# Context attention with heads in row groups, and projections and norms moved in among the steps of self-attention

## The chip, the cores and the metric

The kernel runs on one core of one Trainium2 chip. The metric is the device time of a whole execution in microseconds (us), as the median of several runs: 6629.17 us for the kernel before (3 runs, 6628.52 to 6630.94).

## The reference

A decoder of four layers, pre-norm, in float32. The state x has 2 batches of 1024 tokens of 256 features; a context has 2 batches of 154 tokens. Each layer has three stages, each added onto x: a token mixer, a stage that reads the context, and a feed-forward stage. Four stages are touched by the change. Three hold a self-attention of 16 heads of 16 features:

```python
# L0_attn (causal; keys and values through a latent of 64)
c_kv = x @ W_DKV
k = (c_kv @ W_UK).reshape(b, t, h, hd); v = (c_kv @ W_UV).reshape(b, t, h, hd)
q = (x @ W_UQ).reshape(b, t, h, hd)
probs = softmax(where(causal, einsum('bqhd,bkhd->bhqk', q, k) / sqrt(hd), -inf))
return einsum('bhqk,bkhd->bqhd', probs, v).reshape(b, t, d) @ W_O

# L2_ffn: h = x + attention(rmsnorm(x, ln1_w)); then a mixture of experts on h
# L3_ffn: attention on a layer norm with gain and bias, biases on q, k, v and output;
#         then a mixture of experts
```

The fourth is the context attention of layer 1, 16 heads of 16 features, queries from x, keys and values from the context's 154 tokens:

```python
# L1_xattn: Q = layernorm(x), K = V = ctx
q, k, v = split_heads(Q, Wq, bq), split_heads(K, Wk, bk), split_heads(V, Wv, bv)
attn = softmax(einsum('bhqd,bhkd->bhqk', q, k) / sqrt(d_k), axis=-1)
out = einsum('bhqk,bhkd->bqhd', attn, v).transpose(0, 2, 1, 3).reshape(B, Sq, d_model)
return out @ Wo.T + bo
```

## The kernel before, in words

x stays in SBUF as 16 tiles of 128 tokens (NT = 16; BT = 8 tiles a batch). The program is one list of stages, and each stage takes its tile pools, works and releases them. Inside `attention` a manual schedule holds: each engine's instructions run in the order in which the code issues them.

**Self-attention, `attend` (line 564).** A loop over two batches. For each batch, one after the other: `normed` computes the norm of the batch's eight tiles on VectorE (statistics L250, L251; square root on ScalarE L258; reciprocal; scaling L262 or L264) and turns them with 16 transposes on TensorE (L276), evacuated at L280, L282 or by `evac` (L229 on ScalarE and L233 on VectorE in turn). `heads_T` (line 550) then projects queries and keys, transposed: 8 + 8 groups `hT` of 512 tokens, one for each block `ch` of 128 rows, in which each of four heads has 32 rows (16 features, a row for the maximum, and zeros). L0_attn projects its latent `c` before. Eight value tiles `pv` follow. All of them are matmuls recorded under `mm`, L239.

Then comes `attention` (line 357), with the softmax in two passes. It works in eight steps: two blocks of 512 queries times four groups `ch` of four heads. For each step, the A pass computes scores `sa` with queries on the partitions (L387; one head uses 32 of TensorE's 128 rows) and takes their maxima on VectorE (L416). `m_columns` (L424, L426) puts the negated maxima into a tile M, and `m_rows` (four transposes L432, an add L434) puts them as an extra row beside the queries, so that the B pass's scores `sb` (keys on the partitions, L387) already have the maximum subtracted. ScalarE takes the exponential into `pT` (L447), in the causal stage GpSimd clears the upper triangle (L450), and the value matmuls (L461) accumulate `o`, copied to `oT` (L466). After the last group of a query block, four `finish` calls transpose, divide by the sums and project the output (L340, L342, L344, L318, then `po` L239, and the add to x L326).

The order is written by hand. All of step 0's maxima and four more pairs go ahead of the first B score; this stretch is called the lead below. Then the A pairs of step i + 1 are spread between the B pairs of step i. A tick follows each pair, and a list `due` counts ticks down for what comes later:

```python
LEAD, LAG, KB, FIN, STEP, GAP = 4, 3, 2, 3, 1, 2
...
first = len(a_items(0)) + LEAD
while na < first:
    it = a_next()
    a_matmul(it, 0)
    a_matmul(it, 1)
    tick()
```

Scores of both passes share a pool of seven PSUM banks; `o` has one bank. `pT` has six buffers.

**Context attention, `context_attention` (line 1088).** It serves L1_xattn and L3_xattn. It norms all 16 tiles, projects queries into two blocks of 128 rows (eight heads of 16 features each), and writes keys block-diagonally into `kbd` (L1116, L1118): a key block holds one head's 16 rows and zeros elsewhere. Then it runs over 64 units, a token tile times a group of four heads, in a software pipeline: `front` computes scores `s` (L1148, two matmuls of 128x308, two heads each, over all 128 rows), the maximum (L1160), the subtraction (L1161) and the exponential (L1162); `middle`, two units later, transposes the weights `p` (L1171, eight transposes in two tiles `pt`) and copies them to `pT`; `back` multiplies by the values (L1181, eight matmuls into 32 rows each). `finish` is the same as above. GpSimd adds the output bias to x in `add_row` (L299).

Of the kernel before, what the change touches and what calls it, by code (L numbers as in the profile page):

```python
# [8 lines left out]
F32 = mybir.dt.float32  # L9
# [62 lines left out]
def _blocks(f):  # L72
# [15 lines left out]
    for i in range(2):  # L88
# [8 lines left out]
    g = "L1_xattn_"  # L97
    put("b4", q=_kp(f[g + "Wq"].T), k=_kp(f[g + "Wk"].T), v=_kp(f[g + "Wv"].T), o=_kp(f[g + "Wo"].T),
        bq=_col(f[g + "bq"]), bk=_col(f[g + "bk"]), bv=_row(f[g + "bv"]), bo=_row(f[g + "bo"]))
    g = "L1_ffn_"  # L100
# [73 lines left out]
class Model:  # L174
# [110 lines left out]

    def normed(self, pool, psum, eps=1e-5, g=None, b=None, rms=False, src=None, twice=False, t0=0, n=NT):

        xT = pool.tile([P, 2, n * P], F32, name="xT")
        with self.tc.tile_pool(name="xn", bufs=1) as xp:
            xn = xp.tile([P, n, D], F32, name="xn")  # L290
            self.norm(xp, (self.x if src is None else src)[:, t0 : t0 + n, :], xn, n, eps, rms)
            if twice:
                self.norm(xp, xn, xn, n, eps, rms)
            self.transposed(psum, xn, xT, n, g=g, b=b)
        return xT
# [60 lines left out]

    def attention(self, b, qT, kT, v, causal, wo, x):

# [12 lines left out]
        with ExitStack() as c:  # L371
            pool = lambda name, bufs, **kw: c.enter_context(tc.tile_pool(name=name, bufs=bufs, **kw))
            sb = pool("att", 2)
            pa = pb = pool("att_a", 7, space=PSUM)
            po_pool = pool("att_o", 1, space=PSUM)
            steps = [(qb, ch) for qb in range(S // QB) for ch in range(4)]
            M = []
            for i in range(2):
                m = sb.tile([P, QT, P], F32, name=f"M{i}", bufs=1)
                nc.gpsimd.memset(m, 0.0)  # L380
                M.append(m)
            nk = lambda qb: (qb + 1) * QT if causal else BT
            mms, pTs, os, oTs = {}, {}, {}, {}
# [5 lines left out]
            def a_items(i):  # L389
                qb, ch = steps[i]  # L390
                out = []
                for t in range(QT):
                    qt = qb * QT + t
                    n = (qt + 1) * P if causal else S
                    for half, k0 in enumerate(range(0, n, 512)):
                        for hp in range(2):
                            out.append((i, t, half, k0, min(n, k0 + 512), hp, (n + 511) // 512))
                return out
# [5 lines left out]
            def a_matmul(item, j):  # L404
                i, t, half, k0, k1, hp, halves = item
                qb, ch = steps[i]
                if i not in mms:
                    mms[i] = self.small.tile([P, QT, 2, 4], F32, name="mm", bufs=3)
                n, h = k1 - k0, 2 * hp + j
                s = pa.tile([P, 512], F32, name="sa", tag="sb")[:, :n]  # L410
                q0 = (qb * QT + t) * P
                score(s, qT, kT, h, ch, q0, q0 + P, k0, k1)
                if causal and half == halves - 1:
                    d = s[:, n - P :]
                    nc.vector.tensor_tensor(d, d, self.c["tri"], ALU.add)
                nc.vector.tensor_reduce(mms[i][:, t, half, h : h + 1], s, AX.X, ALU.max, negate=True)  # L416

            def m_columns(i):
# [3 lines left out]
                cols = m.rearrange("p t (j r) -> p t j r", j=4)[:, :, :, DH]  # L422
                if causal and qb == 0:
                    nc.vector.tensor_copy(cols, mm[:, :, 0, :])  # L424
# [11 lines left out]
            def b_matmul(item, j):  # L436
# [4 lines left out]
                if j == 0 and hp == 1:  # L441
                    pTs[i, kc] = sb.tile([P, 4, QB], F32, name="pT", bufs=6)
                h = 2 * hp + j
                s = pb.tile([P, QB], F32, name="sb", tag="sb")
                score(s[:, :n], kT, qT, h, ch, kc * P, kc * P + P, q0, q0 + n)
                p = pTs[i, kc]
                nc.scalar.activation(p[:, h, :n], s[:, :n], AF.Exp)  # L447
                if causal and kc * P >= qb * QB and j == 1:
# [3 lines left out]
            def values(i, kcs):  # L452
# [4 lines left out]
                for kc in kcs:  # L457
                    p = pTs.pop((i, kc))
                    n = (qb + 1) * QB - max(qb * QB, kc * P) if causal else QB
                    for j in range(4):  # L460
                        nc.tensor.matmul(os[i][32 * j : 32 * j + 32, QB - n :], v[:, kc, 4 * ch + j, :], p[:, j, :n],  # L461
                                         start=kc == 0, stop=kc == last)
# [21 lines left out]

            LEAD, LAG, KB, FIN, STEP, GAP = 4, 3, 2, 3, 1, 2
            A = [it for i in range(len(steps)) for it in a_items(i)]
# [24 lines left out]

            with tc.manual_schedule():
                first = len(a_items(0)) + LEAD
                while na < first:
                    it = a_next()
                    a_matmul(it, 0)
                    a_matmul(it, 1)
                    tick()
                goal = first
                for i, (qb, ch) in enumerate(steps):  # L520
# [3 lines left out]
                    for g, bi in enumerate(B):  # L524
                        goal = base + share * (g + 1) // len(B)
                        its = []
                        while na < min(goal, len(A)):
                            its.append(a_next())
                        it = its[0] if its else None
                        for j in range(2):  # L530
                            if it:
                                a_matmul(it, j)
                            b_matmul(bi, j)
                        for it in its[1:]:
                            a_matmul(it, 0)
                            a_matmul(it, 1)
                        if g % 2:
# [25 lines left out]

    def attend(self, name, make, wq, wk, wv, wo, x, causal=False, bq=None, bk=None, bv=None):

        nc, tc = self.nc, self.tc
        for b in range(B):
            with ExitStack() as c:  # L570
                sb = c.enter_context(tc.tile_pool(name=f"{name}{b}", bufs=1))
                qT = sb.tile([P, 4, S], F32, name="qT")
                kT = sb.tile([P, 4, S], F32, name="kT")
                v = sb.tile([P, BT, H, 32], F32, name="v")
                nc.gpsimd.memset(v, 0.0)
                nc.gpsimd.memset(v[:, :, :, DH], 1.0)
                with tc.tile_pool(name=f"{name}{b}p", bufs=3, space=PSUM) as psum, tc.tile_pool(name=f"{name}{b}x", bufs=1) as xp:
                    qs, kv = make(b, xp, psum)
                    kparts = kv[0].shape[0]
                    self.heads_T(psum, qT, wq, qs, 0, S, 0.25, bq)  # L580
                    self.heads_T(psum, kT, wk, kv, 0, S, None, self.c["one16"] if bk is None else bk, kparts)
                    for t in range(BT):
                        pv = psum.tile([P, D], F32, name="pv", tag="tp")
                        self.mm(pv, [(xk[:, t * P : t * P + P], w[:kparts]) for xk, w in zip(kv, wv)])
                        pvh = pv.rearrange("p (h d) -> p h d", h=H)
                        if bv is None:
                            self.evac(v[:, t, :, :DH], pvh)
                        else:
                            nc.vector.tensor_tensor(v[:, t, :, :DH], pvh, bv.rearrange("p (h d) -> p h d", h=H), ALU.add)
                self.attention(b, qT, kT, v, causal, wo, x)  # L590

    def of_normed(self, **kw):


        def make(b, pool, psum):
            xT = self.normed(pool, psum, t0=b * BT, n=BT, **kw)
            chunks = [xT[:, k, :] for k in range(2)]
            return chunks, chunks

        return make  # L600

    def L0_attn(self):
        w = self.weights("b0")

        def make(b, pool, psum):
            xT = self.normed(pool, psum, t0=b * BT, n=BT)
            ckv = pool.tile([64, S], F32, name="ckv")
            for t0 in range(0, S, 512):  # L610
                ps = psum.tile([64, 512], F32, name="c", tag="tp")
                self.mm(ps, [(w["dkv"][:, k * 64 : k * 64 + 64], xT[:, k, t0 : t0 + 512]) for k in range(2)])
                self.evac(ckv[:, t0 : t0 + 512], ps)
            return [xT[:, k, :] for k in range(2)], [ckv]

        self.attend("l0a", make, [w["uq"][:, :512], w["uq"][:, 512:]], [w["uk"]], [w["uv"]], w["o"], self.x, causal=True)

# [585 lines left out]
    def L1_xattn(self):  # L1203
        self.context_attention(self.weights("b4"))

# [56 lines left out]
    def L2_ffn(self):  # L1262
# [3 lines left out]
        with tc.tile_pool(name="l2f", bufs=1) as sb:  # L1266
            h = sb.tile([P, NT, D], F32, name="h0")
            with tc.tile_pool(name="l2f_n", bufs=1) as np_:
                self.norm(np_, self.x, h, NT, 1e-5)
            self.attend("l2f", self.of_normed(src=h, rms=True, g=w["g1"]), cut(w["q"]), cut(w["k"]), cut(w["v"]), w["o"], h)  # L1270
            self.L2_experts(w, h)
# [313 lines left out]
    def L3_ffn(self):  # L1585
# [3 lines left out]
        with ExitStack() as top_stack:  # L1589
# [6 lines left out]
            with tc.tile_pool(name="l3f_n", bufs=1) as np_:  # L1596
                self.norm(np_, self.x, x1, NT, 1e-5)
            self.attend("l3f", self.of_normed(src=x1, g=w["g1"], b=w["b1"]), cut(w["q"]), cut(w["k"]), cut(w["v"]), w["o"], x1,
                        bq=w["bq"], bk=w["bk"], bv=w["bv"])
# [470 lines left out]
```

## Time and profile before

| what | value |
|---|---|
| median of 3 runs | 6629.17 us |
| profiled execution: its own time | 6639.63 us |
| profiled execution: span in the trace | 6637.7 us |
| TensorE (PE) busy | 5827.5 us, 88% of the span |
| VectorE (DVE) busy | 3994.5 us, 60% |
| ScalarE (ACT) busy | 2786.3 us, 42% |
| GpSimd (POOL) busy | 1462.3 us, 22% |
| L0_attn, latent of batch 0 to its first B score | 16.04 to 60.33 us |
| L1_xattn, first transpose to last output projection | 2103.47 to 2354.71 us |
| L2_ffn batch 0, first transpose to last output projection | 3828.63 to 4131.46 us |
| L2_ffn, first projection of batch 1 | 4142.77 us |
| L3_ffn, last output projection of batch 0, first projection of batch 1 | 5945.45, 5955.44 us |

The profile is one execution. Its span is the time from the first to the last instruction in the trace, and 1.9 us of the execution lie around it. A line "L387" is line 387 of the kernel before; a helper's line collects all stages that call it, so a stage is picked out by a window of time or by the names of the tiles. "out<-in" names the tiles of an instruction, "128*128 128x512" the weights and the moving operand of a matmul. A float32 matmul leaves two records. "[0.61 <-DVE v L233]" behind a group is the idle time before it and the instruction that ended that time. PEclk is the TensorE clock that was granted, as a share of full speed.

### The profile page before, as it was taken

The numbers are of one execution on the slowest core, as the hardware profiler recorded it, in microseconds if no ns is written. First come the engines' busy times: TensorE is split into PE (matmuls) and PEld (weight loads), VectorE is DVE, ScalarE is ACT, GpSimd is POOL, SyncE is SP. The second block draws the span as 40 slices with busy tenths as digits, with TensorE's granted clock in tenths as the row PEclk, the third lists the DMA queues.
The fourth block names the chain that finished last, engine by engine and source line by source line (L and its number), as shares of the span: only waits on it lengthen the run. The fifth ranks groups of instructions, "written<-read, shape, count | busy, mean of one in ns | idle before, by whom it ended". The sixth has DMA issues, their size and how long they took to land.

```text
span 6637.7 us, 79839 instructions
## 1 busy us (share of the span) xinstructions
PE 5827.5 (88%) x30196; PEld 3190.3 (48%) x30196; DVE 3994.5 (60%) x7906; ACT 2786.3 (42%) x5377; POOL 1462.3 (22%) x1095
## 2 busy tenths in 40 slices
PE   8898999999998987787878799988687987999896
PEld 4445656565644653333324544445444445444464
DVE  7665545454556735998983365652376778657521
ACT  3344545454501416787762035441133433354411
POOL 1110000000002005998992100001323133000012
PEclk8899999999988998998989789988878898999888
DMA  1000000000000003554551000011100000000022
GB/s 38 1 1 15 1 1 1 14 1 1 1 10 23 1 14 98 143 146 130 151 150 44 13 1 1 1 64 67 53 1 13 1 6 16 1 1 1 13 84 94
DMA packets 112621, 234.88 MB, mean 35 GB/s; under 512 B 12965, under 2 KB 37133, under 8 KB 108525
## 3 DMA queue, kind: packets, MB, share of 16 engines
q1 hardware_dynamic: 97872, 194.73, 10.0%
q0 software_dynamic: 6480, 17.70, 0.9%
q10 hardware_dynamic: 7884, 17.34, 0.7%
q8 instruction: 239, 3.92, 0.2%
q14 instruction: 146, 1.19, 0.1%
HBM read 211.51 MB, written 18.22 MB: 35 GB/s over the span
## 4 chain that ended last, share of the span: by engine, by line
PE 38%; DVE 11%; POOL 4%; ACT 3%; issue 3%; DMA 2%; DVEq 0%; POOLq 0%; ACTq 0%; SPq 0%
PE sb L387 7%; PE sa L387 6%; PE po L239 5%; PE o L461 5%; PE pa L239 4%; DVE bx L1959 2%; DVE mm L416 2%; PE hT L239 2%; PE y L1982 2%; POOL bx L1945 1%; PE pb L239 1%; DMA bn<-bc 1%; PE tp L276 1%; DVE hc L1968 1%; PE pv L1806 1%
## 5 line engine op out<-in xcount | busy, mean ns | idle before, releaser
L416 DVE TENSOR_REDUCE mm<-sa 128x1 f32<-128x512 f32 (+3 forms) x1792 | 1037.7, 628 | 280.0 <-PE sb L387 235.3
L447 ACT ACTIVATE pT<-sb 128x512 f32<-128x512 f32 (+3 forms) x1792 | 904.0, 555 | 656.1 <-PE sb L387 478.8
L387 PE MATMUL sb<-qT,kT 32*128 32x512 f32 (+3 forms) x3584 | 1102.6, 604 | 15.4 <-DVE mm L416 9.6
L387 PE MATMUL sa<-kT,qT 32*128 32x512 f32 (+3 forms) x3584 | 1066.7, 633 | 6.9 <-DVE v L233 2.4
L1982 PE MATMUL y<-hc,const 128*128 128x512 f32 x1024 | 509.9, 634 | 109.6 <-POOL hc L1969 86.9
L1945 POOL TENSOR_TENSOR bx<-du,bn 128x1024 f32<-128x1024 f32 x256 | 603.8, 2366 | 1.1 <-ACT a L1950 1.1
L387 PEld LDWEIGHTS sb<-qT,kT 32*128 32x128 f32 x3584 | 431.9, 190 | 337.4 <-DVE mm L416 204.2
L387 PEld LDWEIGHTS sa<-kT,qT 32*128 32x128 f32 x3584 | 460.1, 202 | 270.3 <-issue 128.6
L299 POOL TENSOR_TENSOR x<-x,w_b 128x4096 f32<-128x4096 f32 x6 | 53.2, 8860 | 1939.2 <-DVE xn L264 1674.5
L461 PE MATMUL o<-pT,v 128*32 128x512 f32 (+3 forms) x3584 | 422.1, 587 | 6.2 <-POOL pT L450 3.4
L1950 ACT ACTIVATE a<-delta,A 128x512 f32<-128x512 f32 x512 | 349.2, 688 | 177.5 <-DVE bx L1959 174.2
L763 DVE TENSOR_REDUCE m<-s 128x1 f32<-128x1024 f32 x256 | 312.8, 1222 | 166.9 <-PE s L737 166.9
L793 ACT COPY pT<-pt 128x512 f32<-128x512 f32 x384 | 210.1, 582 | 447.0 <-PE pt L784 447.0
L1982 PEld LDWEIGHTS y<-hc,const 128*128 128x128 f32 x1024 | 199.0, 201 | 397.9 <-issue 199.1
L784 PE MATMUL pt<-const,p 128*128 128x128 f32 (+1 forms) x2560 | 363.9, 281 | 6.8 <-DVE pT L793 3.1
L810 PE MATMUL o<-pT,v 128*64 128x256 f32 (+1 forms) x2560 | 340.1, 391 | 0.0
L1959 DVE TENSOR_TENSOR_SCAN bx<-a,carry,bx 128x512 f32<-128x512 f32 x256 | 315.7, 1269 | 22.4 <-POOL bx L1945 12.8
L1959 DVE TENSOR_TENSOR_SCAN bx<-a,bx 128x512 f32<-128x512 f32 x256 | 300.8, 1209 | 46.0 <-POOL bx L1945 27.2
L784 PEld LDWEIGHTS pt<-const,p 128*128 128x128 f32 (+1 forms) x2560 | 265.5, 136 | 129.0 <-issue 115.4
L276 PE MATMUL tp<-const,xn 128*128 128x128 f32 x416 | 103.3, 420 | 235.3 <-DVE xn L264 156.9
L768 ACT ACTIVATE p<-s,m 128x1024 f32<-128x1024 f32 x256 | 287.0, 1121 | 53.9 <-DVE m L764 53.4
L1969 POOL TENSOR_TENSOR hc<-bx,cn 128x512 f32<-128x512 f32 x224 | 286.6, 1279 | 30.5 <-issue 15.3
(463 smaller groups left out, 9167.7 us busy)
## 6 DMA issues: line engine op xcount, KB each, us to landing
bn<-bc SPq DMA_DIRECT2D x256, 256.0 KB, 3.3
cn<-bc SPq DMA_DIRECT2D x256, 256.0 KB, 3.6
w_b<-b SPq DMA_DIRECT2D x10, 2052.0 KB, 9.4
up<-b ACTq DMA_DIRECT2D x8, 1024.0 KB, 16.6
yd<-y SPq DMA_DIRECT2D x39, 128.0 KB, 1.7
xs<-xn SPq DMA_DIRECT2D x8, 512.0 KB, 3.8
down<-b ACTq DMA_DIRECT2D x8, 512.0 KB, 5.5
yd<-ye SPq DMA_DIRECT2D x8, 512.0 KB, 2.9
```

What stands on the lines that cost most here:

```text
L239: self.nc.tensor.matmul(out, lhsT, rhs, start=i == 0, stop=i == len(pairs) - 1)
L387: nc.tensor.matmul(s, lhs[r, ch, l0:l1], rhs[r, ch, r0:r1], start=True, stop=True)
L416: nc.vector.tensor_reduce(mms[i][:, t, half, h : h + 1], s, AX.X, ALU.max, negate=True)
L447: nc.scalar.activation(p[:, h, :n], s[:, :n], AF.Exp)
L461: nc.tensor.matmul(os[i][32 * j : 32 * j + 32, QB - n :], v[:, kc, 4 * ch + j, :], p[:, j, :n], start=kc == 0, stop=kc == last)
L763: nc.vector.tensor_reduce(m[:, 1:2], s1, AX.X, ALU.min)
L784: nc.tensor.transpose(pt[:n, k, :], p[j][:, kc * P : kc * P + n], self.ident)
L810: nc.tensor.matmul(o[64 * j : 64 * j + 64, :], v[:n, k, h * 64 : h * 64 + 64], pT[:n, k, j, :, :].rearrange("p t q -> p (t q)"), start=k = ...
L1945: nc.gpsimd.tensor_tensor(bx, dus[i, c0], bns.pop(k).unsqueeze(1).to_broadcast([P, 2, TB]), ALU.mult)
L1950: nc.scalar.activation(decays[k, j], deltas[i, c0][:, j, :], AF.Exp, scale=A[:, c0 + j, n : n + 1])
L1959: nc.vector.tensor_tensor_scan(run(bx[:, j, :]), run(a), run(bx[:, j, :]), h0, ALU.mult, ALU.add)
L1982: nc.tensor.matmul(y[:, j, :], ident, hc[:, j, :], start=False, stop=n == 15)
```

## The change

1. `L1_xattn` no longer calls `context_attention`. It pads its heads to 32 rows in the packed weights and calls `attention` with 154 keys (`short`). In that mode the A pass of a step is four items of which two issue work: eight scores of 128x154 into four banks, two tiles of tokens in each, and four reductions over 128x2x154. The B pass has two key blocks a step, of 128 and 26 rows. Step 0 and step 1's maxima make its lead. Batch 0's projections go `first` or `beside` the lead's maxima; batch 1's queries, keys and values go `within` batch 0's steps. L3_xattn still calls `context_attention`.
2. `attend` takes one set of PSUM pools for both batches, in place of one for projections and one for attention in each batch. Ahead of a batch's maxima go only the latent (L0_attn) and the query and two key groups of row group 0 that step 0 needs; the 13 other projections and eight value tiles are issued between the lead's pairs of maxima, about one a pair. They are evacuated on ScalarE (values with a bias on VectorE); before, the two engines took turns or VectorE did it.
3. Batch 1's norm is cut into 21 parts (`norm_parts`), and these are issued `within` batch 0's steps, one every second tick from the eighth on.
4. `pT` has five buffers, not six.

The diff, cut to its core:

```diff
     g = "L1_xattn_"
-    put("b4", q=_kp(f[g + "Wq"].T), k=_kp(f[g + "Wk"].T), v=_kp(f[g + "Wv"].T), o=_kp(f[g + "Wo"].T),
+    put("b4", q=_kp(_heads32(f[g + "Wq"].T)), k=_kp(_heads32(f[g + "Wk"].T)), v=_kp(f[g + "Wv"].T), o=_kp(f[g + "Wo"].T),
...
-    def attention(self, b, qT, kT, v, causal, wo, x):
+    def attention(self, b, qT, kT, v, causal, wo, x, psum=None, first=(), beside=(), within=(), keys=S):
...
-            pa = pb = pool("att_a", 7, space=PSUM)
-            po_pool = pool("att_o", 1, space=PSUM)
+            pb, po_pool = psum or (pool("att_a", 7, space=PSUM), pool("att_o", 1, space=PSUM))
+            pa = pb
...
+            short = keys <= 256
+            nk = lambda qb: (qb + 1) * QT if causal else -(-keys // P)
+            rows = lambda kc: min(P, keys - kc * P)
...
+                if short:
+                    return [(i, t, 0, 0, keys, hp, 1) for t in range(0, QT, 2) for hp in range(2)]
...
+                if short:
+                    if hp == 0 and j == 0:
+                        four = [pa.tile([P, 512], F32, name="sa", tag="sb")[:, : 2 * n] for _ in range(4)]
+                        for k in range(2):
+                            q0 = (qb * QT + t + k) * P
+                            for h in range(4):
+                                score(four[h][:, k * n : k * n + n], qT, kT, h, ch, q0, q0 + P, 0, n)
+                        for h in range(4):
+                            nc.vector.tensor_reduce(mms[i][:, t : t + 2, 0, h], four[h].rearrange("p (t k) -> p t k", t=2), AX.X, ALU.max, negate=True)
+                    return
...
-                    pTs[i, kc] = sb.tile([P, 4, QB], F32, name="pT", bufs=6)
+                    pTs[i, kc] = sb.tile([P, 4, QB], F32, name="pT", bufs=5)
...
+            LEAD, LAG, KB, FIN, STEP, GAP, PACE = 4, 3, 2, 3, 1, 2, 2
+            if short:
+                LEAD, LAG = 4, 4
...
+                for f in first:
+                    f()
+                start = len(a_items(0)) + LEAD
+                while na < start:
                     it = a_next()
                     a_matmul(it, 0)
                     a_matmul(it, 1)
                     tick()
+                    for _ in range(-(-len(beside) // (start - na + 1))):
+                        beside.pop(0)()
+                for k, f in enumerate(within):
+                    due.append([8 + PACE * k, f])
...
+                        if short:
+                            for it in its:
+                                held.append(it)
+                            if g % 2:
+                                for it in held:
+                                    a_matmul(it, 0)
+                                    a_matmul(it, 1)
+                                held.clear()
+                                for bi in B[g - 1 : g + 1]:
+                                    b_matmul(bi, 0)
+                                    b_matmul(bi, 1)
...
+    def norm_parts(self, b, src, xn, xT, nn, psum, tag, eps=1e-5, rms=False, g=None, gb=None):
...
+        parts = [lambda t=t: statistics(t) for t in range(BT)] + [rstd]
+        for h in range(2):
+            parts += [lambda t=t: scaled(t) for t in range(4 * h, 4 * h + 4)]
+            parts += [lambda k=k, h=h: turned(k, h) for k in range(2)]
+        return parts
+
+    def attend(self, name, wq, wk, wv, wo, x, src=None, causal=False, bq=None, bk=None, bv=None, down=None, **kw):
...
+            pb, po = pool("p", 7, space=PSUM), pool("o", 1, space=PSUM)
...
+            norms = [self.norm_parts(b, src, xn, xT, nn, pb, "sb", **kw) for b in range(B)]
+            with tc.manual_schedule():
+                for f in norms[0]:
+                    f()
+            for b in range(B):
+                first = [lambda t0=t0: lower(t0) for t0 in (0, 512)] if down is not None else []
+                of = lambda ch: [lambda: query(ch, 0), lambda: key(ch, 0), lambda: key(ch, 512)]
+                first += of(0)
+                beside = of(1) + [lambda t=t: value(t) for t in range(BT)] + of(2) + of(3)
+                beside += [lambda ch=ch: query(ch, 512) for ch in range(4)]
+                self.attention(b, qT, kT, v, causal, wo, x, (pb, po), first, beside, norms[1] if b == 0 else [])
...
     def L1_xattn(self):
-        self.context_attention(self.weights("b4"))
...
+            xT = self.normed(sb, pb, tag="sb")
+            self.add_row(self.x, w["bo"])
...
+            for b in range(B):
+                c0 = b * S
+                of = lambda ch: [lambda: query(ch, c0), lambda: key(b, ch)]
+                first = of(0) if b == 0 else []
+                beside = of(1) + [lambda i=i: value(b, i) for i in range(2)] + of(2) + of(3) + [lambda ch=ch: query(ch, c0 + 512) for ch in range(4)]
+                within = [lambda t0=t0, ch=ch: query(ch, t0) for t0 in (S, S + 512) for ch in range(4)] + [lambda ch=ch: key(1, ch) for ch in range(4)]
+                within += [lambda i=i: value(1, i) for i in range(2)]
+                self.attention(b, qT[:, :, c0 : c0 + S], kT[:, b], v[:, b], False, w["o"], self.x, (pb, po),
+                               first, beside if b == 0 else [], within if b == 0 else [], keys=SC)
```

`query`, `key`, `value` and `lower` are the old projections cut into one group a call. `statistics`, `rstd`, `scaled` and `turned` inside `norm_parts` hold the instructions of `norm` and `transposed`.

## The prediction

> **What bounds the kernel now.** I read the page first, then stretches of the windows view, then the timeline of TensorE around the stages that change.
>
> ```profile
> span 6637.7 us, 79839 instructions
> PE 5827.5 (88%) x30196; PEld 3190.3 (48%) x30196; DVE 3994.5 (60%) x7906; ACT 2786.3 (42%) x5377; POOL 1462.3 (22%) x1095
> ...
> L416 DVE TENSOR_REDUCE mm<-sa 128x1 f32<-128x512 f32 (+3 forms) x1792 | 1037.7, 628 | 280.0 <-PE sb L387 235.3
> L447 ACT ACTIVATE pT<-sb 128x512 f32<-128x512 f32 (+3 forms) x1792 | 904.0, 555 | 656.1 <-PE sb L387 478.8
> ```
>
> PE is the bound as a whole, but the four stages of the change have phases of their own. The windows view shows them (PE, PEld, DVE, ACT, POOL busy, then the granted clock):
>
> ```profile
> core 0: us, PE busy (x) PEld busy (x) DVE busy (x) ACT busy (x) POOL busy (x), PEclk, DMA share, GB/s
> 3832.40:3867.00 34.60, 34.42 (x97) 17.94 (x95) 11.00 (x18) 3.88 (x8) 0.07 (x1) 1.00 0.00 0
> 3867.40:3892.00 24.60, 23.35 (x86) 14.69 (x86) 22.00 (x38) 0.00 (x0) 0.53 (x2) 0.62 0.00 1
> 3895.00:4095.00 200.00, 200.00 (x1333) 86.37 (x1330) 140.86 (x241) 123.71 (x223) 0.00 (x0) 1.00 0.00 1
> 2137.50:2356.80 219.30, 215.76 (x1952) 141.21 (x1952) 159.04 (x255) 90.53 (x144) 0.00 (x0) 0.98 0.01 1
> ```
>
> Rows 1 to 3 are one batch of L2_ffn: projections (PE alone), the first maxima (DVE 89% busy, PE waiting for it), then the steady steps. Row 4 is L1_xattn's main phase, PE-bound. The timeline of PE gives the seams:
>
> ```profile
> 3832.28 27.63 PE L239 MATMUL hT<-xT,w_b 128*128 128x512 f32 x64
> 3859.75 7.07 PE L239 MATMUL pv<-w_b,xT 128*128 128x256 f32 x32
> 3867.43 19.49 PE L387 MATMUL sa<-kT,qT 32*128 32x512 f32 x68 [0.61 <-DVE v L233]
> 3888.13 1.11 PE L432 MATMUL sa<-const,M 128*128 128x128 f32 x4 [1.21 <-DVE M L426]
> 3889.18 4.66 PE L387 MATMUL sa<-kT,qT 32*128 32x512 f32 x15
> 3892.75 1.49 PE L387 MATMUL sb<-qT,kT 32*128 32x512 f32 x3
> ...
> 4139.09 3.88 PE L276 MATMUL tp<-const,xn 128*128 128x128 f32 x16 [7.64 <-DVE xn L262]
> ```
>
> An f32 matmul leaves two records (two passes), so x64 is 16 projections of two matmuls, 1.72 us each; a value tile is 0.87. From transposed input to the first exponential's score is 3832.28 to 3892.75, 60.5 us. The last row is batch 1's norm: PE's last output projection ends at 4131.5 and its next projection starts at 4142.8.
>
> **Part 1, self-attention leads (three stages, two batches each).** The same 16 projections and 8 value tiles remain, but only three projections (query, two keys of row group 0) precede the maxima; 13 projections and 8 value tiles go between the 20 pairs of maxima. PE's single records in the steady phase price a seam: after a 32-row score a full-array matmul starts 0.52 us after the last pass began, against 0.43 within a run, and the first pass after a seam lasts 0.53 instead of 0.43. So a lone pair of 512-column scores costs PE 0.53+0.52 = 1.05, and the way back some 0.15. A pair alone uses two of four row groups, so its partners no longer share its time. Sum for L2 and L3: 20 x 1.05 + 13 x 1.72 + 8 x 0.87 + 20 x 0.15 + 0.5 (transposed maxima) = 53.8; with 3 x 1.72 ahead and 0.9 of eviction latency, 59.9. DVE needs 40 x 0.60 = 24 in that time and is hidden under PE; the evictions (16 x 0.59 on ACT) too. Against 60.5 that is almost nothing; the steps then begin at full clock (the first eight-score group now takes 8.8 instead of 7.2), so I take 1.5 us a batch, 6 in four. Bounds: without any seam 52 (8 a batch gained); with seams of 0.3 more, 12 a batch lost.
> L0_attn is causal: 12 pairs of 128 to 512 columns (about 0.4 to 1.05 each, 8 in all), key projections of one matmul (0.89). Ahead 3.7 + 1.7 + 1.8, then 21.4 of projections and values, 8 + 1.8 for pairs and returns, 0.6, and 1.5 latency: 40.5, against 16.04 to 60.33, 44.3. I take 4 a batch, 8.
>
> [...]
>
> **Part 2, batch 1's norm inside batch 0's steps.** What goes: last projection out to first projection in, 10.4 (L0), 11.3 (L2) and 10.0 (L3, 5945.4 to 5955.4), 31.7 together. What it adds to batch 0: the steps have a direct price list, since the outputs of the first half are finished inside them. The value matmuls start every 7.20 us (3901.56, 3908.76); with one transposed maximum 7.66; with the four finishing tiles 8.25, 11.05 and 9.73, so 7.4 for 7 us of PE work, while 5 us of DVE work in the same tiles cost nothing. So inserted PE work is paid in full and DVE work hides as long as it is spread (DVE idles 1.7 of 7.2). Four groups of transposes: 4 x 0.67 = 2.7. The 8.5 to 11.5 us of DVE come one small part every other tick: hidden, but for the reciprocal, which waits behind a queued Sqrt with its two table loads (1.28 each), and behind it wait the maxima, and PE for their banks: up to 3. I take 5.5 a stage, so the gain is 31.7 - 16.5 = 15. Bounds: 2.7 (DVE all hidden) to 17 (everything in line) a stage: +24 to -19.
>
> **Part 3, L1_xattn.** Now, per head group and token tile:
>
> ```profile
> L1148 PE MATMUL s<-kbd,qT 128*128 128x308 f32 x256 | 84.3, 454 | 4.5 <-DVE v L1125 4.2 <-DVE p L1161 0.3
> L1171 PE MATMUL pt<-const,p 128*26 128x128 f32 x256 | 38.5, 273 | 0.0
> L1171 PE MATMUL pt<-const,p 128*128 128x128 f32 x256 | 38.5, 273 | 0.0
> L1181 PE MATMUL o<-pT,v 128*32 128x128 f32 x512 | 32.9, 285 | 0.3 <-ACT pT L229 0.3
> L1181 PE MATMUL o<-pT,v 26*32 26x128 f32 x512 | 26.9, 280 | 0.1
> ```
>
> Together 3.2 to 3.4 us x 64 units on PE, 219 us; from the first query (2110.35) to the end 246.5. Gone are scores against padded keys, all transposes of the weights and their copies. The new work is 16 steps (a half batch, four heads). A step on PE: 16 scores of 128x154 for the maxima, four row groups at once, 2.0 by the 128-column scores of L0's lead (seven in 0.65) scaled; 8 transposed scores of 512 columns, 1.9 (four in 0.96 by the rows 0.53 + 0.43); 8 value matmuls 1.92; transposed maxima 0.5; five seams 0.6. That is 6.9. Waits: PE reaches the transposed maxima before DVE has done four reductions (128x308 lies between 0.42 and 0.56 in L0's rows: 0.48 each) and the copy, 1.2 us; seven banks serve eight tiles of a half step, so scores wait for ACT's exponentials (0.55 each), some 0.4. A step 8.5.
> Queries double, since heads are padded to 32: 16 x 1.72 instead of 8; keys 8 x 0.6 instead of 4. Lead: three steps' query and key, batch 0's values, the rest of its queries and four maxima groups: 25.4. Batch 0: six steps 51, two without maxima 9, batch 1's eight queries, keys and values within 19.8 (5 of it in the steps' waits), finishing 15.4, last values and wait 4: 94. Batch 1: lead 9 (maxima alone), steps 60, finishing 15.4, end 4: 89. Sum 208.5 against 246.5: 38 gained. DVE (some 65 of 94 in batch 0) and ACT (5.3 of 8.5 a step) stay below PE. Bounds: no wait at all, 175 (71 gained); scores, reductions, exponentials and values strictly in turn, 14 a step, 290 (45 lost). POOL's add of the output bias (8.9 us) stands before the two mask clears that the first transposed maxima need, at about 2118, as early as they are wanted: no cost; were the lead shorter, up to 1 us.
>
> Edits at nothing: five pT buffers for six (the order has three in use at once; covered by the three-tick lag, otherwise 1.2 us of values a pair), the query scale on ACT (idle in the leads), weights of L1_xattn of the same load.
>
> **Sum.** 6 + 8 + 15 + 38 = 67. The profiled execution, 6639.6, becomes 6573; the runs' median lies 10.5 below it, 6629.2, and so **6562**.
>
> **Rivals.**
> *Only the context stage gains* (12%): seams and the Sqrt take all of parts 1 and 2 and the steps of L1_xattn take 10: 20 gained, 6609. For: the L2 and L3 leads already come out even. Against: the regular 0.52.
> *Slower: L1_xattn's steps go in lockstep and the clock halves* (10%). TensorE ran at 0.62 in 3867.40:3892.00 although it counts as busy for 23.35 of 24.60 us: one score on a quarter of the rows per 0.60 us, 36% of the array; the steady steps fill 71% and keep 1.00. A step here fills 4.9 us of array time: 57% of 8.5, but under 40% from 12.3 us on, which it reaches if PE waits for every group of banks in turn. Then PE's 6.9 doubles and steps take 14.5: 14 full steps x 6 and 16 within, 100 lost, 6662. It decides from 13.3 us a step.
> [...]
> *Projections vanish under the maxima* (5%): leads as long as DVE's, 27 + 6 in place of 60: another 90 gained, 6470. Against: PE runs both in turn, as the price list shows.
> *Nothing measurable* (5%): a part given back elsewhere, 6630.
>
> **How the numbers follow.** The forecast has 68%. With the first and third rival it makes faster 0.85; same 0.05; slower 0.10; 0.2% (13 us) is about what a measurement can tell from no change here. The range goes from 6498 (context stage without waits, norm hidden) to 6622 (the first rival with 13 us more lost).
>
> **What would show it.** L1_xattn from its first query to its end near 208 us, steps of 8.5, clock above 0.9; pairs of scores and projections in turn in the leads, 60 us to the first exponential in L2 and 40.5 in L0; 7.20 us between values elsewhere; no gap of 10 us between batches. A lead over 70, steps over 12 or a clock of 0.5 in L1_xattn would make it wrong.

## The result, and the profile after

The changed kernel takes 6568.39 us (median of 4 runs, 6564.68 to 6570.23) where the kernel before takes 6630.06 on the same chip; the ratio is 0.9904, with a 95% interval of 0.9892 to 0.9915. It is 62 us faster, and 6562 was forecast. The page of the changed kernel opens so:

```profile
span 6562.6 us, 78356 instructions
PE 5762.2 (88%) x29540; PEld 3052.2 (47%) x29540; DVE 3865.0 (59%) x7749; ACT 2835.7 (43%) x5487; POOL 1452.0 (22%) x1093
```

Shares of busy time say almost nothing here: TensorE has 88% before and after. The stages say where the time went. This table is read off the two timelines of TensorE, from landmark to landmark (a "lead" runs from the first projection to the first `sb`, "steps" from there to the end of the last output projection, or to the next projection where that starts first; a "gap" is what lies between):

| stretch, us | before | after |
|---|---|---|
| L0_attn: lead, steps of batch 0 | 44.3, 194.1 | 40.8, 198.1 |
| L0_attn: gap, then lead and steps of batch 1 | 10.5, 44.4, 194.3 | 0.0, 39.8, 187.0 |
| L1_xattn: last output projection of L1_attn to first query | 9.2 | 17.5 |
| L1_xattn: first query to last output projection | 246.4 | 207.7 |
| from there to L1_ffn's first transpose | 15.9 | 9.4 |
| L2_ffn: norm ahead of batch 0 | 22.6 | 25.0 |
| L2_ffn: lead, steps of batch 0 | 60.5, 238.7 | 60.5, 245.2 |
| L2_ffn: gap, then batch 1 | 11.3, 299.2 | 0.0, 297.5 |
| L3_ffn: norm ahead of batch 0 | 22.5 | 28.0 |
| L3_ffn: lead, steps of batch 0 | 61.3, 238.7 | 61.6, 248.2 |
| L3_ffn: gap, then batch 1 | 10.0, 298.6 | 0.0, 297.0 |

In L1_xattn before, 2354.71 is where the last output projection starts; it ends at 2356.8, and the table goes to that end. With the 0.8 us by which L0_attn starts later taken off, the changed stretches give 58.4: L1_xattn 37.0, L0_attn 21.1, L2_ffn 4.1, and L3_ffn is 3.8 slower. The two profiled spans differ by 75.1; the other 17 lie in code that is the same in both and are not the change's to claim (the tail of L3_ffn 7.4, the scores of L2_xattn 6.9). The profiled execution of the kernel before was a long one for its kernel (6639.6 us, median 6629), the one after a short one (6564.7, median 6568), so the spans differ by more than the medians.

The timeline of TensorE shows a lead of L2_ffn after the change (start, duration, instruction group):

```profile
3769.30 5.81 PE L239 MATMUL hT<-xT,w_b 128*128 128x512 f32 x12
3775.04 1.13 PE L393 MATMUL sa<-kT,qT 32*128 32x512 f32 x4
3776.10 3.70 PE L239 MATMUL hT<-xT,w_b 128*128 128x512 f32 x8
3779.73 1.13 PE L393 MATMUL sa<-kT,qT 32*128 32x512 f32 x4
```

From a pair of scores to the next projection it is 1.06 us, and two projections take 3.63 to the next pair, twice 1.72 and a seam of 0.19. That is close to the forecast, 1.05 and some 0.15.

A full step of L1_xattn in batch 1:

```profile
2230.23 0.63 PE L450 MATMUL sa<-const,M 128*128 128x128 f32 x4
2230.79 0.81 PE L393 MATMUL sa<-kT,qT 32*128 32x154 f32 x16
2231.43 1.84 PE L393 MATMUL sb<-qT,kT 32*128 32x512 f32 x8
2233.20 2.06 PE L480 MATMUL o<-pT,v 128*32 128x512 f32 x16
2235.19 0.81 PE L393 MATMUL sa<-kT,qT 32*128 32x154 f32 x16
2235.92 1.66 PE L393 MATMUL sb<-qT,kT 32*26 32x512 f32 x8
2238.01 0.63 PE L450 MATMUL sa<-const,M 128*128 128x128 f32 x4 [0.43 <-DVE M L442]
```

It takes 7.78 us, with one wait of 0.43 for VectorE's column of maxima. Where two queries of batch 1 stand inside, a step takes 12.2. The windows view gives the clock over all these steps:

```profile
core 0: us, PE busy (x) PEld busy (x) DVE busy (x) ACT busy (x) POOL busy (x), PEclk, DMA share, GB/s
2121.30:2290.00 168.70, 155.51 (x1192) 72.95 (x1184) 82.83 (x200) 77.42 (x151) 2.83 (x3) 0.96 0.00 1
```

The clock is 0.96 of full speed: the rival of lockstep and a halved clock did not come. (Half the clock is in the trace before: 0.50 from 3877 to 3887 us, in a lead of L2_ffn.) The 40% of the array below which that rival let it fall was the author's estimate, between the 36% that ran at 0.62 and the 71% that ran at 1.00; no run tests it.

### The profile page after: what moved, and what is told of

The parts are those of the page before. It is cut to its first block, busy times and chain, and to the rows that moved or that the text cites. A ratio compares the mean times of both kernels' runs of the same rounds, so it can differ in the third digit from the quotient of the medians.

```text
span 6562.6 us, 78356 instructions
## 1 busy us (share of the span) xinstructions
PE 5762.2 (88%) x29540; PEld 3052.2 (47%) x29540; DVE 3865.0 (59%) x7749; ACT 2835.7 (43%) x5487; POOL 1452.0 (22%) x1093
## 4 chain that ended last, share of the span: by engine, by line
PE 40%; DVE 10%; ACT 4%; POOL 4%; issue 3%; DMA 2%; DVEq 0%; POOLq 0%; ACTq 0%; SPq 0%
PE sb L393 7%; PE sa L393 7%; PE po L239 5%; PE o L480 5%; PE pa L239 4%; DVE bx L2110 2%; PE hT L239 2%; PE y L2133 2%; POOL bx L2096 1%; PE pb L239 1%; DMA bn<-bc 1%; DVE mm L434 1%; ACT a L2101 1%; PE pv L1957 1%; DVE hc L2119 1%
## 5 line engine op out<-in xcount | busy, mean ns | idle before, releaser
L466 ACT ACTIVATE pT<-sb 128x512 f32<-128x512 f32 (+3 forms) x1920 | 968.9, 558 | 722.3 <-PE sb L393 548.3
L393 PE MATMUL sb<-qT,kT 32*128 32x512 f32 (+4 forms) x3840 | 1161.4, 604 | 18.1 <-DVE mm L434 11.8
L393 PE MATMUL sa<-kT,qT 32*128 32x512 f32 (+4 forms) x4096 | 1079.5, 561 | 4.2 <-ACT kT L229 1.4
L393 PEld LDWEIGHTS sb<-qT,kT 32*128 32x128 f32 (+1 forms) x3840 | 443.0, 186 | 366.9 <-DVE mm L434 216.5
L393 PEld LDWEIGHTS sa<-kT,qT 32*128 32x128 f32 x4096 | 436.9, 191 | 308.0 <-issue 180.6
L480 PE MATMUL o<-pT,v 128*32 128x512 f32 (+4 forms) x3840 | 455.8, 588 | 6.5 <-POOL pT L469 3.4
L239 PE MATMUL hT<-xT,w_b 128*128 128x512 f32 x672 | 320.0, 614 | 3.3 <-ACT pT L902 1.4
```

The source lines that it names most:

```text
L239: self.nc.tensor.matmul(out, lhsT, rhs, start=i == 0, stop=i == len(pairs) - 1)
L393: nc.tensor.matmul(s, lhs[r, ch, l0:l1], rhs[r, ch, r0:r1], start=True, stop=True)
L466: nc.scalar.activation(p[:m, h, :n], s[:m, :n], AF.Exp)
L480: nc.tensor.matmul(os[i][32 * j : 32 * j + 32, QB - n :], v[: rows(kc), kc, 4 * ch + j, :], p[: rows(kc), j, :n], start=kc == 0, stop=kc = ...
```

## The experiments

Each kernel was timed in turns with the kernel before on one chip. Ratios are to that kernel, with 95% intervals.

**The two halves of the change.** `ctx_only` has only L1_xattn changed, `self_only` only the three self-attention stages.

```diff
 # ctx_only: the old attend, of_normed and L0_attn; the new L1_xattn
-                    pTs[i, kc] = sb.tile([P, 4, QB], F32, name="pT", bufs=5)
+                    pTs[i, kc] = sb.tile([P, 4, QB], F32, name="pT", bufs=5 if short else 6)
 # self_only: the new attend; the old weights b4 and
     def L1_xattn(self):
+        self.context_attention(self.weights("b4"))
```

> Only L1_xattn is changed; the three self-attention stages are as before. Theory A (the gains add up stage by stage; in the trace the stretch from the last output projection of L1_attn to the first transpose of L1_ffn went from 272.2 to 235.3 us): 37 us under the kernel before, about 6593. Theory B (the prediction's term of 38 less the later start of its norm, 7): 31 under, 6599. Theory C (most of the whole gain comes from self-attention): less than 20 under, above 6610.

> Only the three self-attention stages are changed; L1_xattn is as before. Theory A (stage by stage in the trace: L0_attn 21.1 less, L2_ffn 4.1 less, L3_ffn 3.8 more): 21 us under the kernel before, about 6609, with L3_ffn slower than before. Theory B (the prediction's terms 6 + 8 + 15): 29 under, 6601. The two parts together should give the 62 of the whole change.

`ctx_only` took 6592.82 us, ratio 0.9940 (0.9924 to 0.9957): 40 less. `self_only` took 6604.65, ratio 0.9960 (0.9946 to 0.9974): 28 less. By time alone neither decides between A and B: the intervals reach from 29 to 50 less and from 17 to 36 less. By the traces both are A: the stretch of L1_xattn is 37 us shorter in `ctx_only`, and in `self_only` L0_attn is 20.0 and L2_ffn 4.1 shorter, L3_ffn 2.5 longer. The halves add up to 68 against 62, which is within the intervals. The late start of L1_xattn's norm (17.5 us) is in `ctx_only` and not in `self_only`, so it belongs to the new L1_xattn.

**Batch 1's norm not inside the steps.**

```diff
-                self.attention(..., first, beside, norms[1] if b == 0 else [])
+                self.attention(..., (norms[1] if b else []) + first, beside)
```

> The whole change, but batch 1's norm is issued in one piece ahead of batch 1's projections and not within batch 0's steps. Theory A (the parts cost batch 0's steps 4.0, 6.7 and 9.6 us in the trace, and a norm in one piece costs 10.5 to 12 a stage): 11 to 16 us slower than the whole change, about 6582, and L3_ffn hardly changes. Theory B (VectorE's parts hide under TensorE, as the prediction had it, and only 2.7 of transposes were paid): 24 or more slower, 6592 and above. In this kernel the steady value groups should come every 7.20 us throughout, as in batch 1.

It took 6563.61 us, ratio 0.9899 (0.9882 to 0.9915). Both theories are wrong: it is no slower. By its trace the three stages are 9.9 us shorter than with the norm inside, but 5.2 of that lie in L0_attn and 3.8 in L3_ffn, where the clock differed between the two executions. The steps of batch 0 take 188.9, 237.7 and 237.3 us, so by this comparison the parts inside had cost 9.2, 7.5 and 10.9. Only L2_ffn had a clock of 1.00 in both; the scatter of L0_attn is told under the next kernel, that of L3_ffn under `stats_lead`. Outside, the gap between the batches is only 3.1, 3.6 and 4.0 us. The timeline of TensorE in L2_ffn at the end of batch 0:

```profile
4059.68 1.92 PE L239 MATMUL po<-w_b,onT 128*128 128x256 f32 x8
4061.44 1.04 PE L635 MATMUL tp<-const,xn 128*128 128x128 f32 x8
4063.80 1.56 PE L635 MATMUL tp<-const,xn 128*128 128x128 f32 x8 [1.33 <-DVE xn L628]
```

The transposes follow the last projection at once. The edit did not do all that its description says: the trace shows batch 1's statistics ahead of batch 0's transposes, where they delay batch 0 by 2 to 2.4 us a stage. Before, batch 1's statistics began at 4131.84, after batch 0's last addition. So most of the gap went without the norm inside the steps, and putting it there gained nothing that these runs show. That it went because both batches now share their pools is the likely reason; no run shares the pools and changes nothing else.

**All projections ahead of the maxima.**

```diff
-                self.attention(b, qT, kT, v, causal, wo, x, (pb, po), first, beside, norms[1] if b == 0 else [])
+                self.attention(b, qT, kT, v, causal, wo, x, (pb, po), first + beside, [], norms[1] if b == 0 else [])
```

> The whole change, but all projections and value tiles go ahead of the lead's maxima and none beside them. Theory A (leads are 3.5 us a batch shorter with the projections beside in L0_attn, and in L2_ffn and L3_ffn equal at 60 us, with 1.2 more saved behind them by the full clock): 8 us from L0_attn and 5 from the others, 13 slower than the whole change, 6581. Theory B (switching between full-array and 32-row matmuls eats all that is saved): no change, 6568. Theory C (the maxima are hidden under the projections): over 40 slower.

It took 6591.34 us, ratio 0.9939 (0.9922 to 0.9956): 21 slower than the whole change by its trace, 23 by the medians. Theory A has the right sign and some 60% of the size. L0_attn's leads are back at 44.6, 8.6 longer, as expected; L2_ffn is 7.2 longer, and L3_ffn 2.1 shorter. The last 8 are steps of L0_attn, 4.0 and 3.9 longer, and these are not to be trusted: batch 1's steps there take anything from 186.0 to 194.3 us over the twelve kernels of this study. The windows view shows their second stretch, in this order: the kernel before, the whole change, and `stats_lead` (below), whose batch 1 is the whole change's instruction for instruction.

```profile
340.00:380.00 40.00, 38.75 (x230) 17.32 (x232) 31.26 (x77) 14.83 (x36) 6.91 (x17) 0.80 0.00 1
```

```profile
326.00:366.00 40.00, 38.28 (x262) 19.51 (x261) 36.39 (x89) 15.33 (x39) 7.32 (x18) 0.97 0.00 1
```

```profile
321.40:361.40 40.00, 38.69 (x237) 17.54 (x232) 31.30 (x75) 14.19 (x34) 6.51 (x16) 0.81 0.00 1
```

With the granted clock at 0.97 the steps took 187.0 us, with 0.80 and 0.81 they took 194.3 and 191.6. The old code scatters too: in `ctx_only`, whose L0_attn is that of the kernel before, these steps took 191.7. So some 5 of the 7.3 us that the whole change shows there are the clock's and not shown to be the change's.

**Four heads at a time in the leads.**

```diff
                     a_matmul(it, 1)
+                    if it[5] == 0 and not short:
+                        continue
                     tick()
-                    for _ in range(-(-len(beside) // (start - na + 1))):
+                    for _ in range(-(-len(beside) // (start - na + 1 if short else (start - na) // 2 + 1))):
```

> The whole change, but in the leads of the self-attention stages the two pairs of maxima of one score tile (four heads, four row groups) follow each other directly, and the projections and value tiles come two or three at a time behind them. Theory A (a pair fills only two of TensorE's four row groups, so the second pair's 0.86 us runs in the shadow of the first, and half of the seams of 0.2 us go): 12.5 us less a batch in L2_ffn and L3_ffn (lead 47.5 for 60), 4 to 5 less a batch in L0_attn, 60 in all, about 6508. Theory B (pairs do not share TensorE's time, only seams are saved): 2 us a batch, 10 to 12 in all, 6557. Theory C (VectorE, which now gets four reductions at once, holds the banks): no gain, 6568.

It took 6516.62 us, ratio 0.9826 (0.9809 to 0.9842), 52 under the whole change. Theory A holds: the leads of L2_ffn and L3_ffn are 12.2 to 12.6 us shorter, those of L0_attn 5.8 and 4.8.

```profile
3782.32 1.14 PE L393 MATMUL sa<-kT,qT 32*128 32x512 f32 x8
3783.39 1.99 PE L239 MATMUL pv<-w_b,xT 128*128 128x256 f32 x8
```

Eight records of four heads take 1.07 us to the next projection, where four records of two heads took 1.06. The six leads together are 59.9 us shorter, which is theory A's 60. The span is 49.8 shorter: 4.8 were lost in L0_attn's steps of batch 1, which took 191.8, within the scatter told above; the rest lies in small differences elsewhere.

**Batch 1's statistics beside the lead.**

```diff
+                within = []
+                if b == 0:
+                    for k in range(9):
+                        beside[k + 3] = lambda f=beside[k + 3], g=norms[1][k]: (f(), g())
+                    within = norms[1][9:]
...
```

> The whole change, but the nine parts of batch 1's norm up to the reciprocal root (statistics, square root, reciprocal) are issued beside batch 0's lead and not within its steps; scaling and transposes stay within. Theory A (in the steps these parts cost about 2 us for the statistics and 1.8 in L2_ffn to 5 in L3_ffn for the square root with its two table loads; in the lead VectorE is busy 16 of 40 us and no exponential runs yet, so there they cost nothing): 3.5 less in L2_ffn, 7 in L3_ffn, 3 to 5 in L0_attn, about 6554. Theory B (the parts are paid wherever they stand, since the reductions wait behind them): no change, 6568.

It took 6554.65 us, ratio 0.9888 (0.9871 to 0.9904). Theory A: the steps of batch 0 are 3.8 (L2_ffn) and 7.0 us (L3_ffn) shorter, 4.7 in L0_attn with its scatter, and the leads as long as before (in L0_attn's two, of 40.9 and 39.8 us, VectorE is busy 17.6 and 18.5 in the whole change, not 16). What L3_ffn loses to the square root is seen in the windows view of the whole change and then of this kernel:

```profile
5684.00:5688.00 4.00, 3.10 (x18) 1.65 (x16) 2.35 (x6) 3.73 (x6) 0.00 (x0) 1.00 0.00 0
5688.00:5692.00 4.00, 3.86 (x14) 0.89 (x18) 2.20 (x5) 2.66 (x5) 0.00 (x0) 0.57 0.01 2
5692.00:5696.00 4.00, 4.00 (x22) 1.19 (x14) 0.59 (x1) 0.55 (x2) 0.00 (x0) 0.57 0.00 0
```

```profile
5688.00:5692.00 4.00, 4.00 (x32) 1.80 (x32) 3.86 (x8) 2.17 (x4) 0.00 (x0) 1.00 0.00 0
```

VectorE's reciprocal waited 1.65 us for ScalarE's table load (1.28) and root (0.30), TensorE stood still for 1.04 us behind the maxima, and in the next 8 us it had 0.57 of its clock. That drop is not a fixed price of the stall. The same wait of 1.04 us stands behind the root in the whole change's L2_ffn, and in L3_ffn of `self_only`, `starts`, `lead_fours` and `evac_act`. In `evac_act` (below) the next 8 us ran at full clock, as they did in the whole change's L2_ffn:

```profile
5684.67:5692.67 8.00, 8.00 (x50) 3.23 (x54) 6.00 (x12) 5.82 (x11) 0.00 (x0) 1.00 0.00 1
```

The two value groups around the root then took 1.8 us more than without it, in the whole change 5.1; in `self_only`, whose L3_ffn is the whole change's, and in `starts` it was 3.5. So of the 7.0 us that L3_ffn gains here, some 3 are a drop of the clock that can also stay away.

**Two other starts.**

```diff
-                nc.vector.tensor_scalar(bq4, bq, 0.25, None, ALU.mult)
+                nc.scalar.activation(bq4, bq, AF.Copy, scale=0.25)
...
-            xT = self.normed(sb, pb, tag="sb")
+            with tc.tile_pool(name="l1x_pad", bufs=1) as pad:
+                pad.tile([P, 8192], F32, name="pad")
+                xT = self.normed(sb, pb, tag="sb")
```

> The whole change with two other starts: in L3_ffn the query bias is scaled on ScalarE and not on VectorE, and in L1_xattn the norm's tiles are put 32 KB higher in SBUF. Theory A (VectorE's small scaling waited 3.3 us for GpSimd's clearing of v, and the statistics of L1_xattn waited for tiles of L1_attn that lay at their addresses): L3_ffn from the last output projection to the first query 24.7 for 28.0, L1_xattn 9.2 for 17.5, 11 less in all, 6557. Theory B (the statistics come late because the order of the engines is another one, whatever the addresses; the clearing holds VectorE in any case): no change, 6568.

It took 6556.62 us, ratio 0.9887 (0.9870 to 0.9903). Theory A: L3_ffn's norm takes 25.2 for 28.0, L1_xattn's 9.0 for 17.5. The timeline of the whole change at L3_ffn's start, and then of this kernel:

```profile
5565.87 3.51 POOL L672 MEMSET v<- 128x4096 f32 x1 [13.18 <-DVE x L264]
5566.01 3.40 DVE L677 TENSOR_SCALAR bq<-w_b 128x4 f32<-128x4 f32 x1
```

```profile
5560.09 0.20 ACT L677 ACTIVATE bq<-w_b 128x4 f32<-128x4 f32 x1 [5.67 <-DVE x L264]
5560.12 3.51 POOL L672 MEMSET v<- 128x4096 f32 x1 [13.17 <-DVE x L264]
5560.37 0.18 DVE L613 BATCH_NORM_AGGREGATE norm<-norm 128x2 f32<-128x6 f32 x1
```

Four elements a partition took VectorE 3.40 us while GpSimd cleared `v`. With them on ScalarE, VectorE's statistics run beside the same clearing of 3.51 us, at 0.39 to 0.41 each. In L1_xattn an unused tile of 32 KB was enough: with the norm's tiles 32 KB higher the statistics stand among L1_attn's last additions again, as they did before the change. The traces show no addresses; that L1_attn still used the old ones is inferred from this edit.

**ScalarE's evictions of the turned tiles.**

```diff
-                nc.vector.tensor_scalar(o, i, g[:, k : k + 1], gb[:, k : k + 1], ALU.mult, ALU.add)
+                nc.scalar.activation(o, i, AF.Identity, bias=gb[:, k : k + 1], scale=g[:, k : k + 1])
...
-                nc.vector.tensor_scalar(o, i, g[:, k : k + 1], None, ALU.mult)
+                nc.scalar.activation(o, i, AF.Copy, scale=g[:, k : k + 1])
```

> The whole change, but in L2_ffn and L3_ffn the turned norm tiles (gain, bias) are evacuated on ScalarE and not on VectorE. Theory A (VectorE's work in the steps is paid for about half, since the maxima stand behind it in VectorE's order and TensorE behind the maxima): four evictions of 0.83 us cost 1.7 a stage, 3 less in all, 6565. Theory B (only the transposes on TensorE are paid): no change. Theory C (the exponentials come late behind these evictions): up to 3 more, 6571.

It took 6562.02 us, ratio 0.9896 (0.9880 to 0.9913), which tells nothing by itself. By the trace it is theory B: L2_ffn's steps take 245.2 as before, group for group (8.05, 8.35, 7.46 us). The first norms gain 1.3 us each. L3_ffn's steps take 245.2 for 248.2, but that is the clock behind the root (0.57 there, 1.00 here), which the edit isn't shown to have caused.

**All of it together.** `best` has the last four edits at once; `best_casts` also casts L1_ffn's weights on ScalarE.

> Pairs of maxima four heads at a time in the leads, batch 1's statistics beside the lead, the two mended starts and ScalarE's evictions of the turned norm tiles, all together. Theory A (the gains stand in different stretches and add up: 52 + 14 + 12 + 3 under the whole change): 81 less, 6488. Theory B (the shorter lead, 48 us, no longer hides the statistics: VectorE then has 25 us of maxima and 6 of statistics in it, and the reductions wait): 10 to 15 of it lost again, about 6500.

```diff
 # best_casts, beyond best
-                nc.vector.tensor_copy(f[k], a)
-                nc.gpsimd.tensor_scalar(f[k], f[k], 1.0 / 127.0, None, ALU.mult)
+                nc.scalar.activation(f[k], a, AF.Copy, scale=1.0 / 127.0)
```

> The same, and L1_ffn's weights are turned from int32 to float32 and scaled on ScalarE in one step, and not on VectorE and then GpSimd. Theory A (VectorE's casts stand 0.96 us alone and 4.8 and 4.6 beside GpSimd's scaling, and in the last tiles of L1_xattn TensorE waits 5.0 and 3.4 us for VectorE behind them): L1_xattn from first query to end 8 shorter, about 200 for 207.7; 6480. Theory B (the casts would have filled a wait that is there anyway): no change from the kernel beside it.

`best` took 6494.02 us, ratio 0.9785 (0.9770 to 0.9799), midway between the two theories; its span is 79 us shorter than the whole change's, near theory A's 81. The first leads of L2_ffn and L3_ffn are 50.0 and 51.7 us where they were 48.2 and 49.0 in `lead_fours`, so statistics in a short lead cost 2 to 3 each (a little of theory B). `best_casts` took 6482.68, ratio 0.9771 (0.9757 to 0.9784): the best kernel of this study, 2.3% under the kernel before. L1_xattn from first query to end is 197.6 us for 207.8, as theory A has it. The whole change has these rows at the end of L1_xattn:

```profile
2287.11 0.96 DVE L1408 CAST f_g<-w_b 128x1536 f32<-128x1536 int32 x1 [6.33 <-PE o L480]
2288.17 4.13 POOL L1409 TENSOR_SCALAR f_g<-f_g 128x1536 f32<-128x1536 f32 x1 [72.57 <-DVE f_g L1408]
2288.29 4.83 DVE L1408 CAST f_u<-w_b 128x1536 f32<-128x1536 int32 x1
2293.50 0.69 PE L318 MATMUL onT<-const,on 128*128 128x128 f32 x2 [4.98 <-DVE on L344]
```

A cast that takes 0.96 us alone takes 4.83 beside GpSimd's scaling, and the normalisation of the last tiles waits behind it.

## Why the prediction was right

The total held; its terms did so only in part.

- **L1_xattn, 38 forecast.** First query to end: 208.5 forecast, 207.7 measured, with a lead of 23.7 (25.4 forecast), batch 0 of 93.1 (94) and batch 1 of 90.9 (89). Steps are 7.8 for 8.5. Two terms were missing: the norm's late start, 8.3 lost, and L1_ffn's casts, which left the gap behind the stage 6.5 shorter and went into its last tiles, where TensorE waits 8.4 for them (inside the 90.9).
- **Leads of L2_ffn and L3_ffn, 6 forecast.** The leads stayed at 60 to 61.6, as forecast (59.9), and steps behind them are 1.0 to 1.4 shorter where no norm is inside: about 5 in all. The seam was worth 0.19 us, near the 0.15 to 0.2 of the sum.
- **Leads of L0_attn, 8 forecast.** 3.5 and 4.7 measured, 8.1. Not forecast: shorter steps behind, 7.3 in batch 1 and 5.2 in batch 0 (`norm_serial`, without the norm inside), of which some 5 of the first are the clock's scatter; for the second, `norm_serial` had a clock of 0.94 in these steps and the kernel before 0.89, and no run separates the two.
- **Norm inside, 15 forecast.** This step failed. What goes was right (31.7 forecast and measured). The sum "I take 5.5 a stage" was mis-sized: 9.2, 7.5 and 10.9, 27.6 for 16.5, though inside the stated bounds of 2.7 to 17. Two premises were wrong. VectorE's work did not hide when spread: two statistics parts stretched a group from 7.20 to 7.73, half of their 1.14 us. That was not for want of room: in most steady groups before VectorE idles 2.3 us of 7.2, more than the 1.7 of the forecast. And the root cost 1.8 in L2_ffn, within the forecast's 3, but 5 in L3_ffn, where the clock fell behind it; that part was bad luck of this execution, since `evac_act` has 1.8 there as well (told under `stats_lead`). On top come the first norms, now issued in halves and, in L3_ffn, behind the clearing of `v`: 0.8, 2.4 and 5.5 later.
- **Edits at nothing.** "The query scale on ACT" overlooked the one tiny VectorE instruction that prepares its bias. The row to price it stood in the trace before: the cast `f_d` of L1_ffn, beside GpSimd's scaling, took 4.86 us where `f_g` took 0.95. The fifth `pT` buffer was no loss where the trace can tell: value groups without other work still come every 7.20 us.

So the total of 67 against 62 holds one failed term of about 20: the norm, with its starts, came to 31.7 - 27.6 - 8.7, a loss of 4 to 5 where 15 were to be gained. It is offset by 12 in L0_attn's steps, a good part of which is the clock of this execution. That the total came so near is in part luck.

Two sums of the forecast do not come out of their own terms. No waits in L1_xattn and a hidden norm would give 6520 and not 6498, the lower end of the range; leads of 33 us in place of 60 would gain 108 in four and not 90. Neither decided anything.

The forecast also missed what the lead left lying: it wrote that a lone pair uses two of four row groups, took that as a fixed price, and did not ask for the order that fills all four.

## What to carry to other kernels

When matmuls on a part of the array are interleaved with full ones, put as many of them side by side as there are row groups before switching back (here four heads of 32 rows took 1.07 us to the next projection, two took 1.06); that was worth almost as much here as the whole change, 52 us against 62. Before moving a norm into a loop that is paced by two engines in turn, ask whether letting it slip under the previous tail is enough (here, it seems, the shared pools allowed that: with the norm outside, the gap was 3.1 to 4.0 us for 10.0 to 11.3), and keep a ScalarE function that needs a table load out of the loop where it can stand elsewhere (here the root stood between two loads of 1.28 us and cost 1.8 us in L2_ffn). Check where a rewritten stage's first tiles come to lie in SBUF (8.5 us in L1_xattn), and which small VectorE instructions stand beside a long GpSimd one (3.40 us for four elements a partition).

## What the runs showed of the hardware that was not expected

- Two VectorE instructions that stood beside a GpSimd one ended only after it: a scaling of 128x4 took 3.40 us beside a clearing of 3.51, and a cast 4.83 beside a scaling of 4.13, where the cast of the same shape before it took 0.96. In `starts` statistics took 0.39 to 0.41 beside the same clearing, as they do without it. What sets which instruction is held is open.
- One stall of TensorE of 1.04 us was followed by 8 us at a clock of 0.57, and the same stall in `evac_act` by 8 us at 1.00. What decides between the two is open.
- L2_xattn from its first score to its end, the same instructions in the same order, took 119.2 us before and in `self_only`, and 112.2 to 112.3 in all kernels with the new L1_xattn. In its second 10 us the granted clock was 0.67 before and 0.82 after. What sets which of the two comes is open.
